# Four rearrangements in a four-layer convolution and attention kernel: output products of layer 0, g of two slices, the start of layer 3 and its last gate

## The chip, the cores and the metric

The kernel runs on one core of one Trainium2 chip. The metric is the device time of one execution in microseconds. Before the change three runs took 3419.18, 3421.26 and 3421.86 us, median 3421.26.

A core has five engines that take their instructions each from a queue of its own: TensorE (PE) for matrix products, VectorE (DVE) and ScalarE (ACT) for elementwise work and reductions, GpSimd (POOL), and SyncE (SP), which here only issues DMAs. SBUF is the working memory; PSUM[...] takes what PE computes. An instruction waits on semaphores for what it depends on.

## The reference, cut to what matters

`x` is float32, 4 images of 256 channels and 48 x 48 = 2304 pixels. Four layers each add something computed from the group-normalised `x` (32 groups):

```python
x = x + _L0_conv_ref(_gn(x), ...)  # attention, 8 heads of 64, cosine scores times 10
x = x + _L1_conv_ref(_gn(x), ...)  # pooled, depthwise convs, sigmoid gate on x
x = x + _L2_conv_ref(_gn(x), ...)  # non-local block: one head of 64, then batch norm
x = x + _L3_conv_ref(_gn(x), ...)  # channel gate, depthwise 3x3, instance norm
```

Layer 0 projects q, k, v, computes softmax attention over 2304 positions and an output projection with 256 channels. Layer 2 computes `theta`, `phi` and `g` (64 channels each), `softmax(theta phi / 8) g`, a product with `W_w`, and a batch norm. Layer 3, with SLOPE 0.01:

```python
p = jnp.mean(xw, axis=(2, 3))
h = jax.nn.leaky_relu(p @ attn_w1.T, SLOPE)
a = jax.nn.sigmoid(h @ attn_w2.T)
y = xw * a[:, :, None, None]
y = jax.lax.conv_general_dilated(y, refine_w, window_strides=(1, 1), padding='SAME', feature_group_count=C, dimension_numbers=('NCHW', 'OIHW', 'NCHW'))
y = y + refine_b[None, :, None, None]
mu = jnp.mean(y, axis=(2, 3), keepdims=True)
var = jnp.mean(jnp.square(y - mu), axis=(2, 3), keepdims=True)
y = (y - mu) * jax.lax.rsqrt(var + EPS)
return jax.nn.leaky_relu(y, SLOPE)
```

## The kernel before

The function is `usual_path` (a second path, `general_path`, is for data on which the usual one would not be sound, and does not run here). Each engine executes its instructions in the order in which the Python code records them; this order is written by hand, with slots and ranks.

Layers 0 and 2 are attention in units. In layer 0 a phase is an image b and a pair of heads p; in layer 2 a phase is an image. A unit is one slice of 384 query columns (six slices to an image; in layer 2 two slices side by side, so three units). A unit has nine slots of two key tiles. `attend` runs over the slots; in each it records for PE the scores of this slot (`sc`, L324), for DVE the additions to the row sums of the slot before (`add_up`, `acc`, L373), then what is due in this slot by rank (`fills`), then the products with the values of the slot before (`av`, L344). Fills with a rank below 1 are recorded ahead of `add_up`, the others after it. ACT makes the exponentials `pt` (L330), in eight buffers.

PSUM in these layers: two buffers `sc`, one `av`, two one-bank buffers `pj` for all projections.

- `out_proj` (L743) gives the output projection of one unit of layer 0: two halves of 128 channels, each a product `part` (L759, into `pj`) and an addition `onto` to `x` (L775, DVE). After the last unit of layer 0 (b = 3, p = 3, c = 5) the group norm of image 3 for layer 1 and 2 follows, and layer 2's `project2.start` (L1203, L1209 into `pj`).
- `project2` (L1189) projects for layer 2. `both(s)` (L1239) gives `phi` and `theta` of slice s, which ACT copies to `k` and `q` (L1249); `g(s)` (L1263) makes `g` transposed, 128 x 64 at a time, with 64-row halves, in one `pj` tile of 192 columns, copied by ACT to `v` (L1268). Slices s and s + 3 share a unit's work; for image 0 the slices come from a staged copy, for images 1 to 3 from `x` in SBUF.

Layer 3 has eight tiles, an image n of four and a half k of the channels, and six convolution slots to a tile: slots 0 to 47. A tile's 128 x (50 x 50) padded input lies in `pad`; the nine-tap depthwise convolution is done on PE (L1943) from four shifted copies `sh` of it, where `place` puts the 32-row pieces (L1800 by DMA on SP, L1802 by ACT, L1804 by POOL, L1806 by DVE). `spread_out` gives the pieces that change their rows (all on SP), `keep_here` those that stay; HERE and HERE_LAST say by which engine and how many slots ahead.

The input of a tile is the sum that ends layer 2: the products with `W_w` (`w_product`, L1700) into PSUM, then `grow` (L1762, DVE) scales and adds `x` into `pad`; `square` (L1786, ACT) sums squares for the norm; `border` (POOL, L1771, L1774) fills the edge. `w_tile` is the two-bank tile `w_all`, `cv_tile` one of three two-bank tiles `cv` that also hold the convolutions, `w_pair` a pair of halves of such a tile. `hum` (L200) is a number of products that nothing reads and that keep PE busy.

From the event loop on, each job has a slot and a rank; in each slot the jobs are recorded by rank: FRONT, CONV, PRODUCT, GROW, MID, EVICT, SMALL, MOMENTS, SQUARE, SCALE, LAST, PLACE, STORE. Before the loop, tile 0 and tile 1 are prepared.

A gate (`Chain.steps`) is a chain over two tiles: squares summed (POOL), group sums (PE, L1858), read (ACT, L1862), `pm` (POOL, L1866 to L1870), first layer (PE, L1875), `hidden` (ACT, L1882, to `hraw`), `leaky` (DVE, L1887), second layer (PE, L1892), exponential (ACT, L1899), `rsa` (DVE, L1904 to L1912). Its small PSUM columns are the free end of the second bank of the latest `cv` tile (`g_tile`), which the odd convolution slot writes. GATE_AT gives the slot of each step relative to the image's first slot: 36 for the last image.

A convolution's end is: evicted to `x` by ACT, squared by ACT, `moments` (L1975 to L1982), `scales` (L2003 to L2018) and `shift` (L2024, L2026) for the instance norm, then ACT scales (L2032), DVE leaks and gains (L2038, L2043), SP stores. The last tile takes its statistics straight from PSUM (L1988).

```python
for t in range(min(events), T):
    for _, fn in sorted(events.pop(t, ()), key=lambda job: job[0]):
        fn()
```

Of the kernel before, what the change touches and what calls it, by code (L numbers as in the profile page):

```python
# [14 lines left out]
P = 128  # L15
# [63 lines left out]
def usual_path(  # L79
# [668 lines left out]
    def out_proj(b, p, c, pair, o):  # L748

        cols = slice(c * SL, (c + 1) * SL)  # L750

        of = {}

        def part(k):
            of[k] = ps = pj_tile()
            if k:
                of_out["ps"], of_out["t"] = ps, clock["t"]
            n = SL + (c == 0)
            nc.tensor.matmul(  # L759
                ps[:, :n], lhsT=wo[:, p, k * P : (k + 1) * P], rhs=o["o"][:, :n], start=True,  # L760
                stop=True,
            )

        def onto(k):
            ps, n = of[k], SL + (c == 0)
            if c == 0:
                if k == 0:
                    pair["bo"] = small.tile([P, NK], F32, tag="bo", name="bo", bufs=3)
                bo = pair["bo"][:, k : k + 1]
                if p == 0:  # L770
                    nc.vector.tensor_add(bo, ps[:, SL:n], vec[:, V_BOUT, k : k + 1])
                else:
                    nc.vector.tensor_copy(bo, ps[:, SL:n])
            xs = X[b][:, k, cols]
            nc.vector.scalar_tensor_tensor(  # L775
                xs, ps[:, :SL], pair["bo"][:, k : k + 1], xs, ALU.add, ALU.add
            )

        def first():
            part(0)  # L780
            onto(0)

        soon = b == B - 1 and p == NPAIR - 1 and c == NCH - 2
        return [
            (0.5 if soon else 2.5 if b else 0, first),
            (4, lambda: part(1)), (4.2, lambda: onto(1)),
        ]

    def l0_unit(b, p, c, pair):
# [401 lines left out]
    def project2(b, norm, s2):  # L1191

        at = {}

        def start():
            kd = big.tile([P, N], F32, tag="k", name="kd")
            qv = big.tile([P, N], F32, tag="q", name="qv")
            s2["k"], s2["q"] = kd, qv[:, 0:HALF]
            s2["v"] = qv[:, HALF:N].rearrange("p (j d) -> p j d", d=D)
            ps = pj_tile()  # L1200

            for k in range(NK):
                nc.tensor.matmul(  # L1203
                    ps[:, 0:1], lhsT=w2c[:, k, 0:2, :].rearrange("p t d -> p (t d)"),
                    rhs=norm["nb"][:, k : k + 1], start=k == 0, stop=k == NK - 1,
                )
            for c in HALVES:
                for k in range(NK):
                    nc.tensor.matmul(  # L1209
                        ps[c, 1:2], lhsT=w2c[:, k, 2, :],  # L1210
                        rhs=norm["nb"][:, k : k + 1], start=k == 0, stop=k == NK - 1,
                    )
            bias = small.tile([P, 2], F32, tag="bias2", name="bias2", bufs=3)
            nc.vector.tensor_add(bias, ps[:, 0:2], b2c)
            s2["shift"] = bias[:, 1:2]
            w = wqp.tile([P, NK, 3, P], F32, tag="w", name="w2")
            w = w.rearrange("p k t o -> p k (t o)")[:, :, : 3 * D]
            w = w.rearrange("p k (t d) -> p k t d", d=D)
            for k in range(NK):
                nc.scalar.activation(  # L1220
                    w[:, k], w2c[:, k], AF.Identity, scale=norm["rs"][:, k : k + 1]
                )
            if b:
                at["x"] = lambda s, k: X[b][:, k, s * SL : (s + 1) * SL]
            else:
                at["x"] = lambda s, k: at[s][:, k, :SL]
                fetch(0)
                fetch(1)
            at["w"], at["bias"] = w, bias

        def fetch(s):
            at[s] = xsp.tile([P, NK, SL + 1], F32, tag="xs", name="xs2")
            nc.sync.dma_start(at[s][:, :, :SL], x_out[:, :, s * SL : (s + 1) * SL])

        def both(s):

            ps = pj_tile()[:, :SL]
            for k in range(NK):
                nc.tensor.matmul(  # L1239
                    ps, lhsT=at["w"][:, k, 0:2, :].rearrange("p t d -> p (t d)"),  # L1240
                    rhs=at["x"](s, k), start=k == 0, stop=k == NK - 1,
                )
            phi, theta = HALVES
            cols = slice(s * SL, (s + 1) * SL)
            nc.scalar.activation(
                s2["k"][phi, cols], ps[phi], AF.Identity, bias=at["bias"][phi, 0:1]
            )
            c = s % L2C
            nc.scalar.activation(  # L1249
                s2["q"][HALVES[s // L2C], c * SL : (c + 1) * SL], ps[theta], AF.Identity,  # L1250
                bias=at["bias"][theta, 0:1],
            )
            nc.sync.dma_start(s2["k"][theta, cols], s2["k"][phi, cols])
            if b == 0 and s + 2 < NSL:
                fetch(s + 2)

        def g(s):
            ps = pj_tile()
            nj = SL // P
            for i in range(nj):  # L1260
                for k in range(NK):
                    for c in HALVES:
                        nc.tensor.matmul(  # L1263
                            ps[c, i * D : (i + 1) * D],
                            lhsT=at["x"](s, k)[:, i * P + c.start : i * P + c.stop],
                            rhs=at["w"][:, k, 2, :], start=k == 0, stop=k == NK - 1,
                        )
            nc.scalar.copy(  # L1268
                s2["v"][:, s * nj : (s + 1) * nj, :].rearrange("p j d -> p (j d)"),
                ps[:, : nj * D],  # L1270
            )

        return start, [
            [(1, lambda s=s: both(s)), (2, lambda s=s: g(s))] if b else
            [(1, lambda s=s: g(s)), (2.7, lambda s=s: both(s))] for s in range(NSL)
        ]

# [390 lines left out]
    def w_pair():  # L1668
        both = cv_tile()
        return [both[:, 0, :SL], both[:, 1, :SL]]  # L1670
# [68 lines left out]
    dev = lp.tile([P, B, NK], F32, name="dev")  # L1739
    dev2 = lp.tile([P, B, NK], F32, name="dev2")  # L1740

    for c in range(1, L2C):
        ahead.append(w_pair())
        hum(ahead[c][0][:, :P], 5 if c == 1 else 1)
        w_product(1, c, ahead[c])

    def edges():
# [89 lines left out]
    class Chain:  # L1837
# [5 lines left out]
        def steps(self):  # L1843
# [35 lines left out]

            def hidden():  # L1880
                of["raw"] = small.tile([D, 1], F32, tag="hraw", name="hraw")
                nc.scalar.copy(of["raw"], of["ps"])  # L1882

            def leaky():
                raw = of["raw"]
# [15 lines left out]
            def scaled():  # L1901
# [11 lines left out]

            steps = [
                [(MID, total)], [(SMALL, groups)], [(MOMENTS, read), (MOMENTS, inverse)],
                [(SMALL, first_layer)], [(MOMENTS, hidden)], [(MID, leaky)],
                [(SMALL, second_layer)], [(MOMENTS, gate), (MOMENTS, scaled)],
            ]
            return [
# [3 lines left out]
    class Conv:  # L1923
# [9 lines left out]
        def products(self, s):  # L1933
            g, h = s // 2, s // L2C
            if s % 2 == 0:
                self.ps[g] = cv_last["ps"] = cv_tile()
            out = self.ps[g][:, s % 2, :SL].rearrange("p (r c) -> p r c", c=HW)
            sh = shifted[(2 * self.i + h) % 3].rearrange("p j (r c) -> p j r c", c=W2)
            r0 = (s % L2C) * RS
            for dr in range(3):  # L1940
                for j in range(4):
                    held = slice(0, HELD[j])
                    nc.tensor.matmul(  # L1943
                        out[32 * j : 32 * j + 32], lhsT=made["taps3"][held, self.k, dr, j, :],
                        rhs=sh[held, j, r0 + dr : r0 + dr + RS, 0:HW],
                        start=dr == 0, stop=dr == 2,
                    )
# [134 lines left out]
    def judge():  # L2082
# [21 lines left out]
        return [(0, MID, lows), (2, SMALL, count), (3, MOMENTS, read), (9, LAST, compare)]  # L2104

    GATE_AT = {
        0: (3, 5, 6, 9, 10, 11, 11, 12), B - 1: (-2, 1, 2, 4, 4, 5, 7, 8),
    }
    for n in range(1, B - 1):
        GATE_AT[n] = (-2, 1, 2, 5, 6, 7, 9, 10)  # L2110
# [14 lines left out]
    spread_first(1)  # L2125
    for c in range(L2C):
        square(0, c)
    for c in range(L2C):
        grow(1, c, ahead[c])
        square(1, c)  # L2130
    keep_here(0, 1, (0, 2), "dve")
    noted[0]()
    border(1)


    FRONT, CONV, PRODUCT, GROW, MID, EVICT, SMALL, MOMENTS, SQUARE = range(9)
# [3 lines left out]
    def at(t, rank, fn):  # L2140
        events.setdefault(t, []).append((rank, fn))

    def put_chain(t, parts):
        for dt, rank, fn in parts:
            at(t + dt, rank, fn)

    def put_before(t, i):

        held = {}

        def product(c):
            held[c] = w_product(i, c, w_tile())
# [8 lines left out]
        (-6, 0, (0, 1), "dve"), (-5, 0, (2, 3), "dve"),  # L2161
        (-3, 1, (0,), "act"), (-2, 1, (2,), "act"), (-2, 1, (3,), "dve"), (-1, 1, (1,), "dve"),
    ]
    HERE_LAST = [*HERE[:2], (-3, 1, (0, 1), "act"), (-2, 1, (2, 3), "act")]

    def put_tile(i, t, cv, final):
        for s in range(NSL):
# [18 lines left out]
            return  # L2186
        if i >= len(convs) - 4:
            t += (7, 5)[cv.k]
            at(t + 4, MOMENTS, lambda: cv.moments(nc.vector))
            at(t + 4, MOMENTS, lambda: cv.scales(nc.vector))  # L2190
            at(t + 4, MOMENTS, lambda: cv.shift(nc.vector))
            for g in range(NG3):
                at(t + 5 + g, SCALE, lambda g=g: cv.scale(g))
                u = t + (7, 6)[cv.k] + g
# [913 lines left out]
```

## Time and profile before

| | |
|---|---|
| runs before, us | 3419.18, 3421.26, 3421.86 |
| profiled execution, us | 3420.77 |
| its span, us | 3419.0 |
| granted PE clock, mean | 0.997 |
| layer 0 with layer 1 beside it, us from the start | 0 to about 2880 |
| layer 2 | about 2880 to 3265 |
| layer 3 (first to last convolution product) | 3273.5 to 3400.5 |
| end of the span | 3419.0 |

The page of a profile gives the busy time of each engine, and a chain of work followed back from the last instruction. The costliest groups of instructions are these (busy time, mean ns of one, then the idle time of the engine just before them and what ended most of it):

```profile
L330 ACT ACTIVATE pt<-sc 128x768 f32<-128x768 f32 x1944 | 1473.8, 810 | 746.0 <-PE sc L324 734.4
L373 DVE TENSOR_TENSOR acc<-acc,pt 128x768 f32<-128x768 f32 x1534 | 1527.4, 996 | 177.4 <-ACT pt L330 74.8
L344 PE MATMUL av<-pt,v 64*64 64x384 f32 x13824 | 1274.9, 484 | 0.0
L324 PE MATMUL sc<-q,k 64*64 64x384 f32 x13824 | 1270.1, 482 | 0.5 <-ACT pt L330 0.5
L775 DVE SCALAR_TENSOR_TENSOR x<-pj,bo,x 128x384 f32<-128x384 f32 x192 | 118.4, 617 | 337.7 <-ACT row L391 184.8
```

Lines are those of the kernel before. A busy PE is not PE at its peak: its clock is granted[...]. In a timeline a row joins instructions of one line that follow each other; its length includes the last one's, and the start of the next row gives the step.

### The profile page before, as it was taken

The page shows a single profiled execution, that of the slowest core. Times are in us where ns is not written, and L with a number is a line of the kernel's source. Part 1 is how long each engine was busy: PE and PEld are TensorE (multiplying, and loading weights), DVE is VectorE, ACT ScalarE, POOL GpSimd, SP SyncE. Part 2 cuts the span into 40 slices and gives each one's busy share as a digit, 9 for nine tenths or more (in the row PEclk, how much of TensorE's full clock was granted, in tenths as well). Part 3 has the DMA queues.
Part 4 walks back from the last instruction along what each step waited for, and adds up shares of the span by engine and source line. Part 5 has one row for each costly group of instructions (what it writes and reads, how often), then busy time and mean ns, then how long its engine had stood idle before and what let it go on. Part 6 is the DMA issues. An engine that isn't in the chain of part 4 may idle for free.

```text
span 3419.0 us, 89427 instructions
## 1 busy us (share of the span) xinstructions
PE 3379.3 (99%) x38026; PEld 1679.8 (49%) x38026; DVE 2551.4 (75%) x3427; ACT 2291.0 (67%) x3689; POOL 618.2 (18%) x617
## 2 busy tenths in 40 slices
PE   9999999999999999999999999999999999999998
PEld 5555545555545444555454444554444444444433
DVE  3455645468788888787888787777887888877777
ACT  5565656565786687556875885568857865555576
POOL 3433333321111011001011010011010101121233
PEclk9999999999999999999999999999999999999999
DMA  2211111111111111120111111111111110231067
GB/s 92 50 24 27 22 27 22 27 22 26 22 33 19 26 23 27 26 75 15 32 18 27 22 27 22 27 22 25 22 27 18 26 25 10 46 75 16 9 154 231
DMA packets 111736, 127.05 MB, mean 37 GB/s; under 512 B 42960, under 2 KB 101792, under 8 KB 110560
## 3 DMA queue, kind: packets, MB, share of 16 engines
q1 hardware_dynamic: 110080, 119.34, 17.4%
q8 instruction: 300, 4.92, 0.6%
q10 hardware_dynamic: 1248, 1.91, 0.2%
q14 instruction: 108, 0.88, 0.1%
HBM read 56.99 MB, written 11.80 MB: 20 GB/s over the span
## 4 chain that ended last, share of the span: by engine, by line
PE 91%; DVE 4%; ACT 1%; POOL 1%; issue 1%; SPq 1%; DMA 1%; DVEq 0%; POOLq 0%; ACTq 0%
PE av L344 36%; PE sc L324 35%; PE pj L661 8%; PE pj L759 4%; PE pj L695 4%; DVE acc L373 2%; PE pj L386 1%; PE cv L1943 1%; PE pj L1239 1%; PE pj L1099 1%; DMA sh<-pad 0%; SPq L1800 0%; PE pj L1263 0%; PE pj L1297 0%; SPq L1086 0%
## 5 line engine op out<-in xcount | busy, mean ns | idle before, releaser
L330 ACT ACTIVATE pt<-sc 128x768 f32<-128x768 f32 x1944 | 1473.8, 810 | 746.0 <-PE sc L324 734.4
L373 DVE TENSOR_TENSOR acc<-acc,pt 128x768 f32<-128x768 f32 x1534 | 1527.4, 996 | 177.4 <-ACT pt L330 74.8
L344 PE MATMUL av<-pt,v 64*64 64x384 f32 x13824 | 1274.9, 484 | 0.0
L324 PE MATMUL sc<-q,k 64*64 64x384 f32 x13824 | 1270.1, 482 | 0.5 <-ACT pt L330 0.5
L324 PEld LDWEIGHTS sc<-q,k 64*64 64x64 f32 x13824 | 525.4, 133 | 589.5 <-issue 556.0
L344 PEld LDWEIGHTS av<-pt,v 64*64 64x64 f32 x13824 | 518.1, 133 | 568.5 <-issue 521.5
L424 POOL TENSOR_TENSOR o<-o,rinv 128x384 f32<-128x384 f32 x95 | 121.8, 1283 | 1706.4 <-DMA rinv<-rinv 1696.0
L775 DVE SCALAR_TENSOR_TENSOR x<-pj,bo,x 128x384 f32<-128x384 f32 x192 | 118.4, 617 | 337.7 <-ACT row L391 184.8
L989 ACT ACTIVATE prod<-pd,wt 128x256 f32<-128x256 f32 x486 | 340.7, 762 | 0.2
L661 PE MATMUL pj<-xs,w 128*128 128x384 f32 (+1 forms) x720 | 275.4, 505 | 0.0
L355 POOL TENSOR_TENSOR half<-pt 128x768 f32<-128x768 f32 x96 | 176.2, 1835 | 378.0 <-ACT pt L330 319.9
L661 PEld LDWEIGHTS pj<-xs,w 128*128 128x128 f32 x720 | 124.1, 189 | 127.9 <-ACT v L700 34.3
L373 DVE TENSOR_TENSOR acc<-acc,half 128x768 f32<-128x768 f32 x96 | 91.8, 956 | 120.5 <-POOL half L355 120.2
L1012 DVE TENSOR_REDUCE prod<-prod 128x256 f32<-128x1280 f32 x114 | 168.8, 1480 | 1.0 <-ACT prod L989 1.0
L759 PE MATMUL pj<-o,wo 128*128 128x384 f32 (+1 forms) x384 | 161.8, 503 | 2.8 <-DVE x L775 2.4
L324 PE MATMUL sc<-qv,kd 64*64 64x384 f32 x1728 | 160.3, 485 | 1.5 <-ACT pt L330 1.5
L344 PE MATMUL av<-pt,qv 64*64 64x384 f32 x1728 | 161.5, 489 | 0.0
L367 DVE TENSOR_TENSOR acc<-pt 128x768 f32<-128x768 f32 x108 | 128.0, 1185 | 34.7 <-ACT pt L330 34.6
L695 PEld LDWEIGHTS pj<-w,xs 128*128 128x128 f32 x1080 | 134.4, 191 | 24.2 <-issue 1.2
L695 PE MATMUL pj<-w,xs 128*128 128x128 f32 x1080 | 134.9, 275 | 0.0
L420 POOL TENSOR_TENSOR o<-raw 128x384 f32<-128x384 f32 x95 | 120.8, 1272 | 44.9 <-ACT raw L416 43.8
L416 ACT COPY raw<-av 128x768 f32<-128x768 f32 x108 | 86.4, 800 | 51.1 <-PE av L344 50.1
(316 smaller groups left out, 2124.8 us busy)
## 6 DMA issues: line engine op xcount, KB each, us to landing
xs<-in_x_dram SPq DMA_DIRECT2D x90, 384.0 KB
rinv<-rinv SPq DMA_DIRECT2D x208, 94.5 KB
sh<-pad SPq DMA_DIRECT2D x120, 162.2 KB
out_dram<-x SPq DMA_DIRECT2D x23, 384.0 KB
w<-in_wqkv_dram SPq DMA_DIRECT2D x32, 192.0 KB
x<-in_x_dram SPq DMA_DIRECT2D x4, 1152.0 KB
x<-in_x_dram SPq DMA_DIRECT2D x9, 384.0 KB
rinv<-ls SPq DMA_DIRECT2D x208, 1.5 KB
```

What stands on the lines that cost most here:

```text
L324: nc.tensor.matmul(ps[c * D : (c + 1) * D, h, :SL], lhsT=u["of"]["k"][r, j0 : j0 + D], rhs=u["of"]["q"][r, u["qc"]], start=True, stop=True,)
L330: nc.scalar.activation(pt, ps[:, :, :SL], AF.Exp, scale=u["scale"])
L344: nc.tensor.matmul(u["av"][h * D : (h + 1) * D, half, :SL], lhsT=value(u, j, h)[r], rhs=pt[r, h, :], start=j == 0, stop=j == JB - 1,)
L355: nc.gpsimd.tensor_add(half, pts[0], pts[1])
L367: nc.vector.tensor_add(u["acc"], ready[0], ready[1])
L373: nc.vector.tensor_add(u["acc"], u["acc"], term)
L424: eng.tensor_mul(o, o, u["rinv"])
L661: nc.tensor.matmul(ps[:, :n], lhsT=at["w"][:, k, t, :], rhs=xs[s][:, k, :n], start=k == 0, stop=k == NK - 1,)
L695: nc.tensor.matmul(ps[:, i * P : (i + 1) * P], lhsT=xs[s][:, k, i * P : (i + 1) * P], rhs=at["w"][:, k, 2, :], start=k == 0, stop=k == NK - 1,
L759: nc.tensor.matmul(ps[:, :n], lhsT=wo[:, p, k * P : (k + 1) * P], rhs=o["o"][:, :n], start=True, stop=True,)
L989: nc.scalar.activation(bufs[n % 3][:, :, min(n, 1) + i].rearrange("p (r c) -> p r c", c=AS), pd[:, PAD + dr : PAD + dr + AS, PAD + dc : PA ...
L1012: nc.vector.tensor_reduce(to, bufs[n % 3][:, :, : min(n, 1) + len(taps)], AX.X, ALU.add)
```

## The change

Four parts.

- In `out_proj`, the products and additions of layer 0's last unit get ranks 0.5 and 0.6, so that they are recorded ahead of that slot's `add_up`. Before, the ranks were 2.5, 4 and 4.2; the unit before it already had 0.5 for its first half.
- In `project2`, for images 1 to 3, `g_two(c)` makes `g` of slices c and c + 3 in one `pj` tile of 384 columns and copies them with one ACT instruction. The number of products is the same.
- At layer 3's start, the products and `grow` of tile 1's second and third part, its `border`, its pieces (0, 2), its squares and `noted` move from ahead of the event loop into slots 0 to 2, behind the convolution of slot 0 in the order of ranks. The two `hum` of 5 and 1 (each recorded as two) become one of 12 on the first convolution tile. The third part's product uses `w_tile` instead of `w_pair`. `put_before` for tile 2 comes one slot later.
- In the last gate, first layer, hidden, leaky and second layer go to slots 41, 42, 42 and 43 (before 40, 40, 41 and 43), and `hidden` is a DVE copy at rank MID instead of an ACT copy at MOMENTS. In HERE_LAST the last tile's pieces 2 and 3 of its upper half go by SP instead of DVE. `moments`, `scales` and `shift` of tiles 4 and 5, those of the last image but one, get rank SQUARE in slots 34 and 39 (before MOMENTS in 35 and 39; L1975 to L2026).

```diff
--- before.py
+++ after.py
@@ -780,10 +780,11 @@
             part(0)
             onto(0)
 
-        soon = b == B - 1 and p == NPAIR - 1 and c == NCH - 2
+        end = b == B - 1 and p == NPAIR - 1
         return [
-            (0.5 if soon else 2.5 if b else 0, first),
-            (4, lambda: part(1)), (4.2, lambda: onto(1)),
+            (0.5 if end and c >= NCH - 2 else 2.5 if b else 0, first),
+            *[(0.6 if end and c == NCH - 1 else r, fn)
+              for r, fn in ((4, lambda: part(1)), (4.2, lambda: onto(1)))],
         ]
 
     def l0_unit(b, p, c, pair):
@@ -1270,8 +1271,25 @@
                 ps[:, : nj * D],
             )
 
+        def g_two(c):
+            ps = pj_tile()
+            nj = SL // P
+            for h in range(2):
+                for i in range(nj):
+                    for k in range(NK):
+                        for cc in HALVES:
+                            nc.tensor.matmul(
+                                ps[cc, (h * nj + i) * D : (h * nj + i + 1) * D],
+                                lhsT=at["x"](c + h * L2C, k)[:, i * P + cc.start : i * P + cc.stop],
+                                rhs=at["w"][:, k, 2, :], start=k == 0, stop=k == NK - 1,
+                            )
+            nc.scalar.copy(
+                s2["v"].rearrange("p (h c j) d -> p h c (j d)", h=2, j=nj)[:, :, c, :],
+                ps[:, : 2 * nj * D].rearrange("p (h n) -> p h n", h=2),
+            )
+
         return start, [
-            [(1, lambda s=s: both(s)), (2, lambda s=s: g(s))] if b else
+            [(1, lambda s=s: both(s)), *([(2, lambda s=s: g_two(s))] if s < L2C else [])] if b else
             [(1, lambda s=s: g(s)), (2.7, lambda s=s: both(s))] for s in range(NSL)
         ]
 
@@ -1739,9 +1757,11 @@
     dev = lp.tile([P, B, NK], F32, name="dev")
     dev2 = lp.tile([P, B, NK], F32, name="dev2")
 
-    for c in range(1, L2C):
-        ahead.append(w_pair())
-        hum(ahead[c][0][:, :P], 5 if c == 1 else 1)
+    early = [cv_tile()]
+    hum(early[0][:, 0, :P], 12)
+
+    def second(c):
+        ahead.append(w_pair() if c == 1 else w_tile())
         w_product(1, c, ahead[c])
 
     def edges():
@@ -1879,7 +1899,7 @@
 
             def hidden():
                 of["raw"] = small.tile([D, 1], F32, tag="hraw", name="hraw")
-                nc.scalar.copy(of["raw"], of["ps"])
+                (nc.vector.tensor_copy if self.n == B - 1 else nc.scalar.copy)(of["raw"], of["ps"])
 
             def leaky():
                 raw = of["raw"]
@@ -1913,7 +1933,8 @@
 
             steps = [
                 [(MID, total)], [(SMALL, groups)], [(MOMENTS, read), (MOMENTS, inverse)],
-                [(SMALL, first_layer)], [(MOMENTS, hidden)], [(MID, leaky)],
+                [(SMALL, first_layer)], [(MID if self.n == B - 1 else MOMENTS, hidden)],
+                [(MID, leaky)],
                 [(SMALL, second_layer)], [(MOMENTS, gate), (MOMENTS, scaled)],
             ]
             return [
@@ -1933,7 +1954,7 @@
         def products(self, s):
             g, h = s // 2, s // L2C
             if s % 2 == 0:
-                self.ps[g] = cv_last["ps"] = cv_tile()
+                self.ps[g] = cv_last["ps"] = early.pop() if early else cv_tile()
             out = self.ps[g][:, s % 2, :SL].rearrange("p (r c) -> p r c", c=HW)
             sh = shifted[(2 * self.i + h) % 3].rearrange("p j (r c) -> p j r c", c=W2)
             r0 = (s % L2C) * RS
@@ -2104,7 +2125,7 @@
         return [(0, MID, lows), (2, SMALL, count), (3, MOMENTS, read), (9, LAST, compare)]
 
     GATE_AT = {
-        0: (3, 5, 6, 9, 10, 11, 11, 12), B - 1: (-2, 1, 2, 4, 4, 5, 7, 8),
+        0: (3, 5, 6, 9, 10, 11, 11, 12), B - 1: (-2, 1, 2, 5, 6, 6, 7, 8),
     }
     for n in range(1, B - 1):
         GATE_AT[n] = (-2, 1, 2, 5, 6, 7, 9, 10)
@@ -2125,12 +2146,7 @@
     spread_first(1)
     for c in range(L2C):
         square(0, c)
-    for c in range(L2C):
-        grow(1, c, ahead[c])
-        square(1, c)
-    keep_here(0, 1, (0, 2), "dve")
-    noted[0]()
-    border(1)
+    grow(1, 0, ahead[0])
 
 
     FRONT, CONV, PRODUCT, GROW, MID, EVICT, SMALL, MOMENTS, SQUARE = range(9)
@@ -2140,6 +2156,16 @@
     def at(t, rank, fn):
         events.setdefault(t, []).append((rank, fn))
 
+    for c in range(1, L2C):
+        at(0, PRODUCT, lambda c=c: second(c))
+    for c in range(1, L2C):
+        at(0, GROW, lambda c=c: grow(1, c, ahead[c]))
+    at(0, GROW, lambda: border(1))
+    at(0, GROW, lambda: keep_here(0, 1, (0, 2), "dve"))
+    for c in range(L2C):
+        at(c // 2, SQUARE, lambda c=c: square(1, c))
+    at(2, MID, noted[0])
+
     def put_chain(t, parts):
         for dt, rank, fn in parts:
             at(t + dt, rank, fn)
@@ -2147,6 +2173,7 @@
     def put_before(t, i):
 
         held = {}
+        t += i == 2
 
         def product(c):
             held[c] = w_product(i, c, w_tile())
@@ -2161,7 +2188,9 @@
         (-6, 0, (0, 1), "dve"), (-5, 0, (2, 3), "dve"),
         (-3, 1, (0,), "act"), (-2, 1, (2,), "act"), (-2, 1, (3,), "dve"), (-1, 1, (1,), "dve"),
     ]
-    HERE_LAST = [*HERE[:2], (-3, 1, (0, 1), "act"), (-2, 1, (2, 3), "act")]
+    HERE_LAST = [
+        HERE[0], (-5, 0, (2, 3), "sp"), (-3, 1, (0, 1), "act"), (-2, 1, (2, 3), "act"),
+    ]
 
     def put_tile(i, t, cv, final):
         for s in range(NSL):
@@ -2186,9 +2215,10 @@
             return
         if i >= len(convs) - 4:
             t += (7, 5)[cv.k]
-            at(t + 4, MOMENTS, lambda: cv.moments(nc.vector))
-            at(t + 4, MOMENTS, lambda: cv.scales(nc.vector))
-            at(t + 4, MOMENTS, lambda: cv.shift(nc.vector))
+            u = t + 3 + cv.k
+            at(u, SQUARE, lambda: cv.moments(nc.vector))
+            at(u, SQUARE, lambda: cv.scales(nc.vector))
+            at(u, SQUARE, lambda: cv.shift(nc.vector))
             for g in range(NG3):
                 at(t + 5 + g, SCALE, lambda g=g: cv.scale(g))
                 u = t + (7, 6)[cv.k] + g
```

## The prediction

> **What bounds the kernel now.** I read the page's busy shares first, then its chain of work that ended last, then TensorE's timeline around each of the four places that the diff touches, and last the stretches with a granted clock below 1.
>
> ```profile
> PE 3379.3 (99%) x38026; PEld 1679.8 (49%) x38026; DVE 2551.4 (75%) x3427; ACT 2291.0 (67%) x3689; POOL 618.2 (18%) x617
> PE 91%; DVE 4%; ACT 1%; POOL 1%; issue 1%; SPq 1%; DMA 1%; DVEq 0%; POOLq 0%; ACTq 0%
> ```
>
> TensorE (PE) is busy for 3379.3 of 3419.0 us: all its gaps, with the tail, make 39.7 us. An edit helps if it closes such a gap, or brings matmuls out of a stretch at half clock. So the places are taken one by one.
>
> Layer 0's end, timeline of PE and then of DVE (start, duration, [idle before <- releaser]):
>
> ```profile
> 2874.92 1.56 PE L759 MATMUL pj<-o,wo 128*128 128x384 f32 x4
> 2878.51 0.61 PE L1203 MATMUL pj<-gn_nb,w2c 128*128 128x1 f32 x4 [2.03 <-DVE x L775]
> 2879.38 2.39 PE L344 MATMUL av<-pt,qv 64*64 64x384 f32 x16
> 2881.53 2.35 PE L324 MATMUL sc<-qv,kd 64*64 64x384 f32 x16
> ...
> 2874.26 0.61 DVE L775 SCALAR_TENSOR_TENSOR x<-pj,bo,x 128x384 f32<-128x384 f32 x1
> 2874.78 3.14 DVE L373 TENSOR_TENSOR acc<-acc,pt 128x768 f32<-128x768 f32 x2
> 2877.85 1.13 DVE L775 SCALAR_TENSOR_TENSOR x<-pj,bo,x 128x384 f32<-128x384 f32 x2
> ```
>
> Both `pj` buffers are held until two additions L775 have read them; these stand behind two row-sum additions L373, and PE waits 2.03 us.
>
> A projection step of layer 2, PE:
>
> ```profile
> 2894.38 0.92 PE L1263 MATMUL pj<-w,x 128*64 128x64 f32 x24
> 2895.67 0.92 PE L1263 MATMUL pj<-w,x 128*64 128x64 f32 x24 [0.37 <-ACT qv L1249]
> 2896.52 1.52 PE L344 MATMUL av<-pt,qv 64*64 64x384 f32 x16
> ```
>
> The second 24 products need a second `pj` buffer, which ScalarE (ACT) still reads. Layer 3's start, then its last gate, PE:
>
> ```profile
> 3267.57 1.35 PE L200 MATMUL cv<-gmat 128*128 128x128 f32 x10 [1.28 <-DVE pad L1762]
> 3271.80 0.46 PE L200 MATMUL cv<-gmat 128*128 128x128 f32 x2 [2.07 <-DVE pad L1762]
> 3273.51 3.27 PE L1943 MATMUL cv<-sh,taps 96*32 96x384 f32 x24
> 3280.00 0.88 PE L1700 MATMUL w<-y,Ww 64*64 64x384 f32 x8 [0.35 <-DVE pad L1762]
> ...
> 3380.86 0.39 PE L1875 MATMUL cv<-pm,w 128*64 128x1 f32 x4 [1.28 <-POOL pm L1870]
> 3383.83 8.29 PE L1943 MATMUL cv<-sh,taps 96*32 96x384 f32 x72 [2.58 <-ACT hraw L1882]
> 3392.58 7.95 PE L1943 MATMUL cv<-sh,taps 96*32 96x384 f32 x96
> ```
>
> Busy time by stretch (first PE with its count, PEld, DVE, ACT, POOL, then the granted clock, DMA share, GB/s): after each wait above about 2 us comes a stretch at 0.50.
>
> ```profile
> 2880.00:2883.30 3.30, 3.30 (x24) 1.31 (x20) 3.20 (x5) 0.20 (x1) 0.00 (x0) 0.50 0.00 0
> 3272.40:3275.80 3.40, 3.40 (x24) 0.79 (x20) 3.40 (x6) 3.29 (x7) 3.16 (x6) 0.50 0.84 204
> 3381.60:3388.40 6.80, 4.57 (x32) 1.47 (x36) 6.26 (x14) 6.69 (x10) 0.54 (x1) 0.50 1.02 234
> ```
>
> [...]
>
> **The change, part by part.**
>
> *A, layer 0's last unit.* DVE's order becomes x, x, x, acc, acc for x, acc, acc, x, x; PE's is unchanged and nothing is added. The second product's addition then runs as soon as its four matmuls are done, some 2875.9 to 2876.5, and L1203 starts at about 2876.53 instead of 2878.51: 1.98 us. With no gap, the av and sc groups that follow (steps 2.15 and 2.17 at half clock) take 1.29 each like their neighbours: 1.74. A = 3.7. The row sums come later against PE; their consumers hold eight `pt` buffers and DVE has 3.9 us of gaps before 2943. If that cover failed, the stall would return there; bounds 1.5 and 4.0.
>
> *B, g of two slices in one bank.* The same 48 products go into one `pj` tile, read by one 128x2x192 copy instead of two copies of 192 columns. The step of the 48 is 2.14 us (2894.38 to 2896.52) in each of nine such chunks of layer 2; without the wait for the second buffer a group of 24 issues in 0.78, so 1.6 for both: 0.51 each. ACT saves one instruction's fixed part and the copy can start only after both groups, 0.8 later; `v` is not needed before the next phase. Eight chunks count, 4.1; the third lies beside an output that waits for DMA (L1099, step 2.42 instead of 1.47, at 2970.20), where the gain is lost. Bounds 2.5 and 4.6.
>
> *C, layer 3's start.* The hums L200 of 10 and 2 become one of 12 at 3267.57, done at 3270.64 (0.128 a record at this clock); conv slot 0 follows at once instead of at 3273.51. Its shifted copies `sh` are issued on SP from 3267.25 to 3269.10 and land by about 3270.6. The products of the second tile then come between convs, and each reuses the PSUM tile that DVE's grow (L1762) must have read: the third waits until 3274.66 for grow(1,0), which is queued behind the other DVE work; grow(2,0) ends at about 3281.1, and the product after it waits to there. Listed in order: conv 0 to 3272.75, product to 3273.56, product 3274.66 to 3275.5, conv 1 to 3277.5, product to 3278.35, conv 2 to 3280.4, product 3281.1 to 3282.0, convs 3 to 5 and one more product to 3288.8. Before, this point is 3289.63. C = 0.8: most of the closed gap returns as DVE's bound. At best all three gaps' excess goes, 2.9; at worst the late squares (now spread over slots 0 to 2) and conv 0's wait for copies cost 2: bounds -2 and 2.9.
>
> *D, last gate.* Three things held PE here. First, DVE computes tile 4's moments (3372.09 to 3374.41) behind two output updates and a copy; ACT idles 2.88 us for them, and its reads for the gate come behind. Moved to the front of slot 34, they would run at about 3369.25 to 3371.55, and the gate's mean `pm` be there before L1875, now a slot later: 1.28 gone. Second, `hidden` goes from ACT, where it queues behind 768-column updates, to DVE[...]: 2.58 gone. Third, the half clock of 3381.6 to 3388.4, where 72 records take 8.2 us instead of 5.9: 2.3. The price: two self-copies of tile 7 leave DVE (2 x 0.85) for SP, which is issuing eight of them at 3374.20 to 3379.53, 0.70 apart, landing some 2 us later. Ten end at about 3381.0 and land near 3383.6; conv 40 and 41 are through at 3380.8 and L1875 at 3381.1, so conv 42 waits some 2.4 us, for DMA. By the rows above a wait of this size can cost a half-clock window again, 1.7. PE then ends at 3397.6 instead of 3400.46: 2.8. Without the clock loss DVE's statistics bound, 4.1. I take D = 2.8, since 2.03 and 2.07 us both cost a window; bounds -1 and 4.5. The tail after the last statistics is as before.
>
> *Sum:* 3.7 + 4.1 + 0.8 + 2.8 = 11.4. The profiled execution took 3420.77 (span 3419.0 and 1.8 around it); 3409.4. The median of the runs is 3421.26, which gives 3409.9. I say 3409.6.
>
> **Rivals.**
> 1. D comes to nothing: the ten transfers and the clock take the place of the waits removed. DMA share of 1.00 at 3375 to 3379 speaks for it; the DVE time saved speaks against. 8.6 gained: 3412.4.
> 2. More is gained: C yields 2.9 and D 4.1, with 0.4 more from B's third chunk. The conv at 3273.51 began before the last remainder had landed, so waits go by region, which is for it; DVE busy 3.35 of 3.40 us at 3269 is against. 15.2: 3405.8.
> 3. A's gain is eaten by DVE, which is without gaps from 2880 to 2902, and D and C give nothing: B and a little of A, 5 us: 3416, within what can be told from no change.
> 4. Slower, by one mechanism: conv 42 waits for ten `sh` transfers on one queue. It decides once the spacing exceeds about 0.70 + 11.4/10, i.e. 1.84 us, where the whole sum is lost; at 2.6 us each conv 42 is 19 us later than forecast and the time is 3428.6. For: `sh` transfers landed 6 to 9 us after issue beside a 1152 KB reload at 3347 to 3357. Against: no such reload lies here.
> That the change does not do what it says is small: the PE order of A is untouched, but DVE's is what it is about.
>
> **How the numbers follow.** Chances: forecast 0.55 (its own range 3407 to 3412), rival 1 0.20, rival 2 0.11, rival 3 0.09, rival 4 0.05. 0.2% (6.8 us, what a measurement can tell from no change) puts the bounds at 3414.4 and 3428.1. Faster: 0.55 + 0.20 + 0.11 less 0.02 for the low edge of rival 1, 0.84; same 0.12 (rival 3 with that edge and the mild end of rival 4); slower 0.04. Range 3405.5 to 3415: rivals 1 and 2 lie inside.
>
> **What would show it.** A: the wait of L1203 is gone and the clock is 1 after it. B: the nine groups of 48 step 1.6 us, with no wait on `qv`. C: conv 0 starts 3 us earlier against L1732, and products wait for grow. D: waits on `pm` and `hraw` gone, one on DMA `sh` before conv 42, the last statistics 3 to 4 us earlier against layer 3's start. Wrong if layer 2's stretches keep their length, or if conv 42 waits beyond 5 us.

## The result, and the profile after

The changed kernel takes 3410.76 us, the median of 8 runs (3409.29 to 3412.74), against 3420.88 us for the one before in the same session (8 runs, 3417.53 to 3422.56): ratio 0.9972, 95% interval 0.9961 to 0.9982. It is 10.1 us faster (6 to 13 us by the interval); 3409.6 was forecast. The profiled execution took 3412.74 us, the slowest of the eight, so the two traces show 8.0 us between their spans (3419.0 and 3411.0) and not 10.1. Line numbers below are those of each run's own kernel; in the changed kernel L1203 became L1204, L1099 L1100, L1263 is joined by L1281 (`g_two`), L1700 became L1718, L1762 L1782, L1806 L1826, L1943 L1964.

The busy shares and the chain that ended last, after:

```profile
PE 3376.7 (99%) x38038; PEld 1678.7 (49%) x38038; DVE 2548.5 (75%) x3426; ACT 2289.2 (67%) x3679; POOL 616.8 (18%) x617
PE 93%; DVE 4%; DMA 1%; issue 0%; POOL 0%; SPq 0%; ACT 0%; DVEq 0%; POOLq 0%; ACTq 0%
```

PE's busy time fell by 2.6 us and its gaps by 5.4. Between the start of the run and the tail this trace has no stretch at half clock; before there were three, of 3.41, 3.41 and 6.83 us at a granted clock of 0.50. A convolution product takes 0.485 us in the trace before at a granted clock of 1.00 and 0.847 at 0.50, 1.75 times as long. The change doesn't rule such stretches out: another execution of the same instructions (e5 below, 3413.31 us) has two, at 3119 and 3355 us.

To see where the time went, each group of products in the trace after is set against the same group before. Difference of the starts, in us:

| at (time before) | difference | what lies between |
|---|---|---|
| 2873.5 | +0.12 | |
| 2883.7 | -3.54 | A: layer 0's last unit |
| 2926.3 | -4.72 | two of B's nine steps |
| 3083.0 | -4.04 | four of B's steps, and the waits below |
| 3173.3 | -5.40 | three of B's steps, less 0.4 at 3107 |
| 3289.6 | -6.05 | C: layer 3's start |
| 3364.3 | -4.52 | beside the two reloads of 1152 KB |
| 3392.1 | -7.79 | D: last gate |
| end of span | -8.0 | tail |

A, after, PE and then DVE:

```profile
2876.66 0.61 PE L1204 MATMUL pj<-gn_nb,w2c 128*128 128x1 f32 x4
2877.53 1.52 PE L344 MATMUL av<-pt,qv 64*64 64x384 f32 x16
2878.87 1.47 PE L324 MATMUL sc<-qv,kd 64*64 64x384 f32 x16
...
2875.99 1.26 DVE L775 SCALAR_TENSOR_TENSOR x<-pj,bo,x 128x384 f32<-128x384 f32 x2 [1.01 <-PE pj L759]
2877.17 2.23 DVE L373 TENSOR_TENSOR acc<-acc,pt 128x768 f32<-128x768 f32 x2
```

The products of layer 2's start no longer wait for the additions, and the groups behind them step 1.34 and 1.29 us, not 2.15 and 2.17.

B, after. First a step, then the places where the lead is given back (PE, PE, ACT, POOL, SP):

```profile
2890.84 1.62 PE L1281 MATMUL pj<-w,x 128*64 128x64 f32 x48
2892.39 1.52 PE L344 MATMUL av<-pt,qv 64*64 64x384 f32 x16
...
2965.24 3.09 PE L1100 MATMUL pj<-y,diag 128*32 128x256 f32 x24
...
3006.83 1.58 PE L324 MATMUL sc<-qv,kd 64*64 64x384 f32 x16 [1.65 <-ACT pt L330]
...
3005.48 0.60 ACT L973 ACTIVATE pd<-blur,gn_nb,rs 128x256 f32<-128x256 f32 x1 [3.86 <-POOL pd L970]
...
3004.69 0.75 POOL L970 MEMSET pd<- 128x784 f32 x1 [5.86 <-DMA stack<-pd]
...
2991.38 11.62 SPq L1087 DMA_DIRECT2D stack<-pd  x16
```

A step of 48 is 1.55 us (2890.84 to 2892.39), 0.59 less than before, in all nine chunks. ACT's copy of 384 columns takes 0.48 us; the two of 192 before took 0.32 each. But the chain to read from the bottom up is this: SP issues 16 `stack` DMAs of layer 1's last branch, one by one, in 11.6 us; POOL may clear `pd` only when they have read it; ACT fills `pd`; and the exponentials for PE stand behind that in ACT's queue. PE came 4.95 us earlier to this place than before, and left it 3.87 earlier. The products on `y`, which wait for DMAs of the same kind, take a step of 3.37 instead of 3.02 at 2944, 3.03 instead of 2.42 at 2965, and 2.46 instead of 1.48 at 3076.5. With 0.4 at 3107, where PE waits for exponentials behind VectorE's additions, 3.4 us of the lead are given back.

This figure belongs to one execution. The runs e3, e4, e5, e7 and e10 below have the same instructions up to 3149 us or later. By 3115 us their traces have given back 1.7, 2.4, 2.0, 1.8 and 0.8 us at the same places, and their waits at `pd` are 1.02, 1.33, 0.75, 0.85 and 0.89 us instead of 1.65. The trace after is the extreme one of the six.

C, after, PE:

```profile
3262.16 2.92 PE L200 MATMUL cv<-gmat 128*128 128x128 f32 x24 [1.28 <-DVE pad L1782]
3265.27 2.38 PE L1964 MATMUL cv<-sh,taps 96*32 96x384 f32 x24 [0.19 <-ACT sh L1822]
3269.22 0.88 PE L1718 MATMUL w<-y,Ww 64*64 64x384 f32 x8 [0.77 <-DVE pad L1782]
3275.79 0.88 PE L1718 MATMUL w<-y,Ww 64*64 64x384 f32 x8 [0.74 <-DVE pad L1782]
```

The wait of 2.07 us and the half clock behind it are gone. Two waits for `grow`, 1.5 us together, came in their place, where before there was one of 0.35.

D, after, PE:

```profile
3368.47 7.95 PE L1964 MATMUL cv<-sh,taps 96*32 96x384 f32 x96
3376.35 0.39 PE L1895 MATMUL cv<-pm,w 128*64 128x1 f32 x4
3376.67 0.83 PE L1964 MATMUL cv<-sh,taps 96*32 96x384 f32 x2
3378.34 0.81 PE L1964 MATMUL cv<-sh,taps 96*32 96x384 f32 x2 [0.83 <-DMA sh<-pad]
3379.61 4.72 PE L1964 MATMUL cv<-sh,taps 128*32 128x384 f32 x44 [0.47 <-DMA sh<-pad]
3384.26 0.60 PE L1912 MATMUL cv<-hl,w 64*128 64x1 f32 x4
3384.79 7.95 PE L1964 MATMUL cv<-sh,taps 96*32 96x384 f32 x96
```

The waits on `pm` and on `hraw` are gone. Conv slot 42 waits for the last tile's DMAs: the profile shows 1.3 us of idle PE, but the price is higher. The 48 products of slots 42 and 43 take 7.59 us (3376.67 to 3384.26), while 96 products in the slots before take 7.88. So 3.65 us are lost: up to 3380.27 six products run one after another, with the idle time between them, and later products start four at a time.

### The profile page after: what moved, and what is told of

It is laid out like the page before. It is cut to its first block, busy times and chain, and to the rows that moved or that the text cites. A ratio compares the mean times of both kernels' runs of the same rounds, so it can differ in the third digit from the quotient of the medians.

```text
span 3411.0 us, 89437 instructions
## 1 busy us (share of the span) xinstructions
PE 3376.7 (99%) x38038; PEld 1678.7 (49%) x38038; DVE 2548.5 (75%) x3426; ACT 2289.2 (67%) x3679; POOL 616.8 (18%) x617
## 3 DMA queue, kind: packets, MB, share of 16 engines
q10 hardware_dynamic: 1248, 1.91, 0.2%
## 4 chain that ended last, share of the span: by engine, by line
PE 93%; DVE 4%; DMA 1%; issue 0%; POOL 0%; SPq 0%; ACT 0%; DVEq 0%; POOLq 0%; ACTq 0%
PE av L344 36%; PE sc L324 36%; PE pj L661 8%; PE pj L759 4%; PE pj L695 4%; PE cv L1964 2%; DVE acc L373 1%; PE pj L386 1%; PE pj L1240 1%; PE pj L1100 1%; DMA sh<-pad 1%; PE pj L1281 0%; PE pj L1315 0%; SPq L1087 0%; DMA x<-x_out 0%
```

## The experiments

Times are medians; each session has its own runs of the kernel before, at 3420.2 to 3420.6.

**Each part undone.**

```diff
 e1: ranks of layer 0's last unit as before (2.5 or 0.5, 4, 4.2)
-            *[(0.6 if end and c == NCH - 1 else r, fn)
-              for r, fn in ((4, lambda: part(1)), (4.2, lambda: onto(1)))],
+            (4, lambda: part(1)), (4.2, lambda: onto(1)),
 e2: g of each slice by itself
-            [(1, lambda s=s: both(s)), *([(2, lambda s=s: g_two(s))] if s < L2C else [])] if b else
+            [(1, lambda s=s: both(s)), (2, lambda s=s: g(s))] if b else
 e3: the hunks of layer 3's start taken out
 e4: GATE_AT, hidden, HERE_LAST and the moments' slots as before
```

> The changed kernel with layer 0's last output products and additions back in their old ranks; all else as changed. Changed kernel: 10.1 us below the one before by the medians. Theory (part of each lead is taken back where the SP queue paces layer 1's last branch, 2954 to 3079 us): the wait of 2 us on the additions and the half-clock window after it return, 3.7 us lost there, but less is taken back afterwards (about 1 to 1.5 us instead of 2.7), so the end is only 2 to 2.5 us later than changed: about 8 us below before. The lead at the start of layer 3 in the trace is then about 3.5 to 4 us instead of 5.4. Rival (parts simply add): 3.7 us later, 6.4 us below before.

Measured: 3414.82 (19 runs, 3410.42 to 3418.67), ratio to before 0.9983 (0.9976 to 0.9990); 4.1 us later than changed, near the rival's 3.7. In the profiled execution the wait is back to the hundredth, but no half clock follows it:

```profile
2878.89 0.61 PE L1203 MATMUL pj<-gn_nb,w2c 128*128 128x1 f32 x4 [2.03 <-DVE x L775]
2879.76 1.52 PE L344 MATMUL av<-pt,qv 64*64 64x384 f32 x16
```

This execution took 3412.27, one of the shortest of the 19, and has one half-clock stretch elsewhere, at 3353. By an estimate from the traces before and after, such a stretch takes 0.0005 off the mean clock of a run (half of 3.41 us in 3411) and the tail's 6.3 us at 0.50 take 0.0009, so 0.999 leaves room for one. The five runs at 0.999 have a median of 3412.27, the twelve at 0.998 of 3415.07 and the two at 0.997 of 3418.5. So about 1.5 of the 4.1 us are there at the clock of the changed kernel, and the rest goes with lower clocks; in which places they fell in those runs is not recorded. The lead at layer 3's start was 6.0 us against my 3.5 to 4, so in this trace B kept 4.7 of its 5.3 us when A was gone. That agrees with a give-back that depends on the lead, but does not show it: e10's trace has the whole lead and gave back little more, 0.8 us by 3115. The total speaks against it.

> The changed kernel with g of each slice in a bank of its own again (two copies instead of one); all else as changed. Theory (leads are taken back in the stretches that the SP queue paces): nine steps of 48 products go from 1.55 to 2.14 us, 5.3 us lost, of which about 3 come back as smaller waits there: 2 to 2.5 us later than changed, about 8 us below before; the lead at layer 3's start is about 3 us. Rival (parts add, each chunk's 0.59 us counts): 5.3 us later, about 5 us below before.

Measured: 3414.42 (13 runs), ratio 0.9982 (0.9974 to 0.9990); 3.7 us later than changed, between the two. All runs have a mean clock of 0.999, which leaves room for one half-clock stretch each, and the trace has none before the tail; so this is waiting time in the main. The lead after A is 3.70 and at 3110 us 2.23.

> The changed kernel with layer 3's start as before (second tile's products and hums ahead of the first slot). Theory (the closed gap comes back as waits for VectorE's grow): 0.7 us later than changed, 9.4 us below before. Rival 1 (the half-clock window at the first convolution slot falls away for good only with this part): 2 to 3 us later, 7 to 8 below before. Rival 2 (this part costs, since squares and copies come later): 1 us earlier than changed.

Measured: 3412.52 (9 runs, 3409.29 to 3413.58), ratio 0.9974 (0.9964 to 0.9984); 1.8 us later than changed. The first rival is nearest, but with 1 us of uncertainty the total does not decide. The clock speaks for this rival: the six runs at a mean clock of 0.999 have a median of 3410.5, that of the changed kernel, and the three at 0.998 of 3413.1. In this trace the half clock came back (PE timeline, then busy time by stretch with PE, PEld, DVE, ACT, POOL, granted clock):

```profile
3264.91 0.46 PE L200 MATMUL cv<-gmat 128*128 128x128 f32 x2 [2.06 <-DVE pad L1780]
3266.29 3.59 PE L1962 MATMUL cv<-sh,taps 96*32 96x384 f32 x24
...
3265.90:3269.30 3.40, 3.40 (x24) 0.99 (x24) 3.40 (x7) 3.30 (x7) 3.03 (x6) 0.50 0.86 207
```

A second one follows at 3378.5.

> The changed kernel with the last gate, the last tile's pieces and the moments of tiles 4 and 5 as before. Theory (the waits on pm and hraw, 3.9 us, and a half-clock stretch of 2.3 us return, a wait of 1.3 us on DMA goes): 3.3 us later than changed by the trace, 7 us below before. Rival (VectorE's own work in the tail is the bound, and the waits are slack): under 1 us later, over 9 us below before.

Measured: 3413.75 (11 runs), ratio 0.9981 (0.9972 to 0.9990); 3.0 us later than changed, the theory's figure. Its trace does not show the theory's working. The wait of 2.58 us on `hraw` is back, but that on `pm` is 0.28 instead of 1.28, and no half clock follows. From the group sums (L1878) to the second layer (L1912) PE takes 15.51 us, 0.6 less than in the trace after. This execution took 3411.43, the shortest of the 11 and the only one at a mean clock of 0.999; the other ten are at 0.998 or 0.997. That fits half-clock stretches in those ten. It would mean that what D is worth in most runs is clock, and that its waits were exchanged for others of about the same size; without traces of such runs this is not shown.

The four losses sum to 12.5 us, against 10.1 for the whole; each is uncertain by about 1 us or more. So the sum says no more than that A, B and D are worth something; C's 1.8 is hardly clear of the uncertainty.

**A known lag.** Twelve idle products, `hum(ps[:, :P], 12)`, ahead of one `g_two`, to see whether a lag is taken back as a lead is.

> The changed kernel with 12 idle products (24 records, 3.1 us on TensorE at full clock) ahead of the first of the nine two-slice g groups, at 2891 us: a loss of known size, put ahead of the stretches that the SP queue and the POOL memset of layer 1's last branch pace (2954 to 3079 us). Theory (a lead is taken back there in part, so a lag is too): the end comes 1 to 2 us later than changed, 3412 to 3412.8 us. Rival (each microsecond on TensorE counts): 3.1 us later, 3413.9.

This was not what ran. The edit counted calls in a list named `twos`, a name that the kernel has for a list of four; the count began at five, the idle products never came, and every engine's instructions are those of the changed kernel. The run is a repeat of it: 3410.02 (6 runs, 3409.84 to 3413.31), 0.7 from 3410.76, which is one measure of what sessions differ by.

> The same 12 idle products ahead of the seventh of the nine groups, at 3152 us, behind the paced stretches of layer 2. Theory: only layer 3's stretch beside the reloads (3346 to 3360 us) can take some of it, so 2 to 3.1 us later than changed, 3412.8 to 3413.9, and more than with the products at 2891 us. Rival: as much as there.

For the same reason the products came ahead of the third group, at 2953 us, and not of the seventh. Measured: 3417.35 (21 runs, 3410.27 to 3421.97), 6.6 us later than changed for 2.9 us of products. The two were repeated with another name for the counter:

> The changed kernel with 12 idle products (24 records, 2.9 to 3.1 us on TensorE) ahead of the first two-slice g group, at 2891 us. In the two runs before that were meant to measure this, the counter had the name of a list that the kernel already has: the first ran the changed kernel's own instructions (3410.0), the second put the products ahead of the third group, at 2953 us, inside the paced stretches, and ended 6.6 us later. Theory (what stands before the paced stretches is taken back in part): 1 to 2 us later than the changed kernel, 3411.8 to 3412.8. Rival 1 (each microsecond counts): 3.1 later, 3413.8. Rival 2 (a lag makes the waits in the paced stretches longer and brings half-clock windows, as at 2953): 5 us or more later.

Measured: 3415.30 (21 runs, 3410.97 to 3420.50), 4.5 us later than changed. My theory said 1 to 2; the second rival is nearest. In the trace the lag is 2.5 us after the products, 0.95 at 2968, so some is taken back, and then it grows:

```profile
3010.05 2.21 PE L324 MATMUL sc<-qv,kd 64*64 64x384 f32 x16 [3.92 <-ACT pt L330]
...
3010.90:3014.30 3.40, 3.40 (x28) 1.44 (x25) 0.72 (x2) 1.62 (x2) 0.00 (x0) 0.50 0.24 53
```

The wait at `pd` is 3.92 us instead of 1.65, and a stretch at half clock follows; two more come at 3342 and 3386. This execution took 3420.50, the longest of the 21, so it shows how a lag can grow and not what is usual. The twelve runs at a mean clock of 0.999 have a median of 3413.0, 2.2 us later than changed for 2.9 us of products, and the nine at lower clocks of 3417.4. In both lagged traces (this one and the one at 2953) POOL's clearing of `pd` comes 14.8 to 14.9 us after the first `stack` issue, in the trace after 13.3, and in those of e3, e4, e5, e7 and e10 12.2 to 12.8. Why these sixteen DMAs take longer then was not found.

> The same idle products ahead of the seventh group, at 3152 us, behind the paced stretches of layer 2. Theory: 2 to 3.1 us later than the changed kernel, 3412.8 to 3413.9; only layer 3's stretch at the reloads can take some back. Rival: a half-clock window falls on other work and adds 1.7.

Measured: 3412.59 (15 runs), 1.8 us later than changed, just under the theory's 2 to 3.1. In its trace the products cost 2.87 us where they stand. What was taken back of them can't be read from it: PE came there 2.84 us earlier than in the trace after, since less of the lead had been given back, and beside the reloads, where the trace after loses, it gains another 3.2 us without any edit there. Then it waits for VectorE's copies of the shifted input:

```profile
3370.19 7.89 PE L1969 MATMUL cv<-sh,taps 96*32 96x384 f32 x70 [2.19 <-DVE sh L1831]
```

**Where the lead is given back.**

```diff
 e7: each reload in three
-            at(t + 18, STORE, lambda k=cv.k: reload(k))
+            for g in range(NG3):
+                at(t + 18 + 2 * g, STORE, lambda k=cv.k, g=g: reload(k, g))
 e8: layer 1's placing DMAs on two queues
-            nc.sync.dma_start(
+            (nc.gpsimd if n % 2 else nc.sync).dma_start(
                 bufs[u][j // 2][32 * q : 32 * q + 32, c0 : c0 + size],
```

> The changed kernel with each of the two 1152 KB reloads of layer 3 cut into three of 384 KB, two slots apart. Theory (shifted copies queue behind the reload on the DMA engines, and this takes 1.5 us of the lead between 3346 and 3360 us): the convolutions there step nearer 2.07 us than 2.7 to 3.2, 1.5 to 3 us earlier than changed, 3408 to 3409.3. Rival (the waits there are VectorE's, or the bytes count whatever their order): no change within 0.7 us.

Measured: 3411.26 (7 runs), no gain: the rival's number. Four of the convolutions beside the reloads step 2.07 us in this trace, and PE gains 1.8 us there on the trace after; but they step 2.07 us in e10's trace too, with the reloads whole, so the gain can't be put down to the edit. PE then meets a wait that the trace after does not have:

```profile
3368.56 6.19 PE L1964 MATMUL cv<-sh,taps 96*32 96x384 f32 x70 [1.64 <-DVE sh L1826]
```

It is the wait of e10: when PE is early, slot 38's four copies on DVE (3.4 us in a row) are the next to be late.

> The changed kernel with every second placing DMA of layer 1's last branch issued by GpSimd instead of SyncE. Theory (these are paced by issue on one queue, 0.69 us each, and that takes back 2.4 us of the lead on the mean of three traces): the products of layer 1 and the exponentials behind pd no longer wait, 1.5 to 2.5 us earlier than changed, 3408.3 to 3409.3. Rival (the transfers themselves or other work pace, or GpSimd's issuing costs more than it brings): no change or 1 to 3 us later.

Measured: 3408.79 (5 runs), ratio to before 0.9965 (0.9951 to 0.9979), 2.0 us earlier than changed, as the theory said, and 1.2 earlier than e5, the changed kernel in the same session. With e12's six, ten of eleven runs on two queues took at most 3409.85; of the fourteen on one queue (the changed kernel's and e5's) three did. POOL and then PE in its trace:

```profile
2999.17 0.75 POOL L970 MEMSET pd<- 128x784 f32 x1 [1.87 <-DMA stack<-pd]
...
2964.94 1.55 PE L1100 MATMUL pj<-y,diag 128*32 128x256 f32 x24
...
3003.48 1.47 PE L324 MATMUL sc<-qv,kd 64*64 64x384 f32 x16
```

No group waits: the products on `y` take 1.47, and the scores after `pd` start on time. Against the trace after, the lead grows by 1.5 us at 2965, 1.8 at 3006 and 1.0 at 3076.5.

> The kernel with layer 1's placing DMAs on two queues (3408.79) and g of each slice in a bank of its own again. Theory (the one queue is what took back part of this edit's gain): now all nine steps of 0.59 us count, 5.3 us later, 3414.1. Rival (something else, say VectorE, took it back): as with one queue, 3.7 us later or less, 3412.5.

```diff
 on e8:
-            [(1, lambda s=s: both(s)), *([(2, lambda s=s: g_two(s))] if s < L2C else [])] if b else
+            [(1, lambda s=s: both(s)), (2, lambda s=s: g(s))] if b else
```

Measured: 3414.13 (20 runs, 3412.75 to 3419.72), 5.3 us later than e8: to the tenth what nine steps of 0.59 give. The tenth is luck: e11's trace is 7.2 us longer than e8's, with a half-clock stretch at 3109, a double one at 3355 and a wait of 4.13 us for `grow` at the reloads. What carries the argument is that in the two traces the distance grows by 0.58 to 0.61 at each of the nine, and that nothing of it is taken back at 2965, 3006 and 3076. With one queue the same edit was worth 3.7. So the one queue is what took back part of B.

> The kernel with layer 1's placing DMAs on two queues, and the last tile's pieces 2 and 3 copied by GpSimd instead of a DMA on SyncE. Theory (conv slot 42 waits 1.3 us for the tenth DMA; GpSimd is idle there and took 1.27 us for such a copy at layer 3's start): about 1.3 us earlier than with two queues alone, 3407.5. Rival (VectorE's copies and updates there contend with GpSimd, and VectorE sets the end): no change or up to 2 us later.

```diff
 on e8, in HERE_LAST:
-        HERE[0], (-5, 0, (2, 3), "sp"), (-3, 1, (0, 1), "act"), (-2, 1, (2, 3), "act"),
+        HERE[0], (-5, 0, (2, 3), "pool"), (-3, 1, (0, 1), "act"), (-2, 1, (2, 3), "act"),
```

Measured: 3408.88 (6 runs), the same as e8; the rival's case. PE, DVE and POOL in its trace:

```profile
3367.81 6.19 PE L1964 MATMUL cv<-sh,taps 96*32 96x384 f32 x70 [1.99 <-DVE sh L1826]
...
3364.14 1.91 DVE L2064 SCALAR_TENSOR_TENSOR x<-pad,bi,x 128x768 f32<-128x768 f32 x1
...
3361.96 3.28 POOL L1824 COPY sh<-pad 32x1298 f32<-32x1298 f32 x2
```

A gain (L2064) that takes 1.02 us elsewhere in this trace takes 1.91 here, where it begins while POOL copies (3361.96 to 3365.24). DVE's four copies begin at 3366.08, in e8's trace at 3364.16, and PE waits for them. That POOL's copies are what lengthens the gain is likely, but not shown. Slots 42 and 43 take 6.07 us instead of e8's 7.67, but the wait of 1.99 us costs as much. So e8 and e12 are the fastest versions that were run, 3408.79 and 3408.88.

## Why the prediction was right, and where it was not

The time was within 1.2 us of the forecast, and all four parts had the sign that was given. By its steps:

- A, 3.7 us: the trace shows 3.66 and the run without it 4.1. The first product of layer 2's start was to begin at 2876.53 and began at 2876.66. What the prediction did not say is that such a wait need not bring the 1.74 of the half clock: without the part, 2.03 us brought it in the trace before and not in e1's.
- B, 4.1 us: the term that was mis-sized. The step was to be about 1.6 and is 1.55, so nine make 5.3, more than the 4.6 put as the bound. (Its own rows, 2.14 less twice 0.78, give 0.58 a step and not the 0.51 that was counted.) Of the places that would take a gain back, one was named, the product on `y` at 2970 (0.6 measured); three more of the same kind, at 2944 (0.35), at `pd` (1.07) and at 3076.5 (0.99), were missed, and VectorE's stretch took 0.4. Net 1.9 in this trace, outside the bounds of 2.5 to 4.6; less was given back in the five other executions of these instructions, and the run without B says 3.7. That 4.1 comes near 3.7 is luck in part, a step too small and a give-back too small. The step that failed is "Eight chunks count": it tested each chunk's neighbours for slack, but not the DMA queue that paces the whole of 2954 to 3079, and e8 and e11 show that this queue took it back.
- C, 0.8 us: 0.65 in the trace, 1.8 by the run without it, whose nine runs span 4.3 us. That the difference is clock is likely by the runs' mean clocks, but which stretch it is stays open, since e3's trace has two. That most of the closed gap comes back as waits for `grow` is seen in the trace: 0.77 and 0.74 us.
- D, 2.8 us: 3.3 in the trace and 3.0 without it. The price was right by luck: conv 42's DMAs cost 3.65 us, not 2.4, and no half clock follows, which had been put at 1.7; 3.65 stands against 4.1. The 2.3 us of the half clock that D was to remove stand in the trace before and not in e4's, and against e4's D gained nothing (15.51 us there, 16.10 in the trace after). Which of D's edits removed the wait of 2.58 on `hraw` was not shown: e4 undoes them together. DMA as the end of this stage was right, with VectorE's copies close behind (e7, e12).
- The lead lost at the reloads, 1.5 us in the trace after, was in no term. Rival 4's mechanism, DMAs late for conv 42, is there, with 3.65 us lost where 11.4 more than the forecast's 2.4 were needed.

The total is nearer than its terms, and that is luck in part: B gave less than its term in the trace, A and D kept theirs, and the runs' median is 2 us below the execution that was profiled.

## What to carry to other kernels

Here, with PE busy for 99% of the span, a closed gap counted only as far as the next stage that something else paces (5.3 us of B's steps, 3.7 in the runs); look for the queue that issues without a break (here SP, 16 issues in 10.5 to 11.7 us) between the edit and the end, and follow it back from the engine whose queue stands behind it. To find the true price of an edit, measure it with that pace removed as well: the same edit was worth 3.7 us with one queue and 5.3 with two. Repeat enough to see the clock: a wait of 2.03 us was followed by 1.74 us of loss at half clock in one trace (before) and by none in another (e1). Take more than one trace of the same kernel before a difference of 1 to 3 us is put down to an edit: here the same places gave back 0.8 to 3.4 us without any. And read the price of a late input from the step of the products as well as from idle time: 1.3 us of idle stood for 3.65.

## What the runs showed of the hardware

- **A wait of some 2 us was followed by half clock in some traces and not in others.** It was after 2.03 us (before, at 2876.5: the next two groups step 2.15 and 2.17 us), 2.07 (before, at 3269.7), 2.06 (e3: 24 products in 3.59 us, the next 24 of the same kind in 2.14) and 2.19 (e10: 70 products in 7.89 us). It was not after 2.03 in e1 (the groups step 1.34 and 1.29), 2.58 in e4 (mean clock 0.999) or 1.99 in e12 (70 products in 6.19 us). The third stretch of the trace before begins at 3381.65, 0.4 us into its wait of 2.58 and behind one of 1.28. So the length of a single wait did not settle it; what does was not shown.
- **A second issuing engine was worth 2 us.** In the trace after SP takes 11.62 us to issue the sixteen `stack` DMAs, and PE waits behind it. With half of such issues on POOL (e8), SP takes 6.21 us for its eight and POOL 2.01 and 2.03 us for four each, and the kernel is 2.0 us faster.
- **A lag cost more than itself in two of three places**: 2.9 us of idle products ahead of the paced stretch or in it cost 4.5 and 6.6 us (e9, e6), behind it 1.8 (e10). Ahead of it, what goes beyond the 2.9 us is found in the runs at a lower mean clock.
